# q and k kept in SBUF in 32 bits, masked by head, in an attention block between two half FFNs

## The chip, the cores and the metric

The kernel runs on one core of a Trainium2 chip. The core has TensorE (matmuls, written to PSUM), VectorE, ScalarE, GpSimd, and SyncE, whose queue (SP) issues most of the DMAs; 16 DMA engines move the data. The metric is the device time of one execution in microseconds: lower is better. Before the change the median of two runs is 1265.03 us (1261.8 and 1268.27).

## The reference

The input x has 8 sequences of 1024 tokens with 256 channels. Three layers are added to it one after another: half an FFN, attention, and half of the same FFN, each on a layer-normalized x.

```
r = sigmoid(xr @ W_r.T);  k = xk @ W_k.T;  ffn = r * (relu(k)**2 @ W_v.T)
        # xr, xk: mu * x + (1 - mu) * (x one token earlier)
q, k, v = split(x @ qkv_w.T + qkv_b)             # 16 heads of 16 dims
for i, o in enumerate(OFFSETS):                  # 40 offsets: 0..32, 48, 64, 96, 128, 192, 256, 384
    lg[i] = (q . k shifted by o) / 4 * (1 + q . scale_embed[i]) + pos_bias[i]
p = softmax(lg over the offsets)                 # offsets before the start are masked
out = sum_i p[i] * (v shifted by o_i) * if_gain
x = x + (out * sigmoid(x @ gate_w.T + gate_b)) @ out_w.T + out_b
```

A token thus attends to itself, the 32 tokens before it, and seven tokens farther back.

## The kernel before, in words

Five stages work on different parts of the tokens at the same time: `f1` (first FFN, in chunks of 256 tokens), `p` (projections, chunks of 256), `qk` (scores, by halves of a sequence, 512 tokens), `att` (softmax, values, output projection, tiles of 128) and `f2` (second FFN). Each stage is a generator; the loop at the end takes their steps in an order given by `TRACE` and gives each step a priority by `RANK`. A scheduler then simulates the engines and writes one fixed instruction order for each engine, so the order on an engine isn't that of the text. PSUM has eight banks, one buffer each: `psa` and `psb` for the FFNs, `psp` for the projections, `psq` for scores, `gp`, `pv`, `pst` for transposes in `att`, and `psy` for the transposed output and the output projection.

The steps that the change touches:

- **Projections** (`stage_p`). `proj(w)` computes a 256 x 256 product from two-part operands in fp32r, twelve matmuls into `psp`. For q and k, ScalarE writes `p + bias` in 16 bits (L263), and VectorE the remainder, also in 16 bits (L264); both go in `hl`. Two DMAs per `hl` (L270) write the parts to DRAM (`qk_d`), in an order in which 32 dims of two heads fill 128 partitions, four rows to a dim.
- **Loads for scores** (`stage_qk`). For each half, q is read back as `qst` (L317), two tiles for the two groups `g`, and k in `kb` (L319), which holds the whole sequence, with zeros where the other head of a pair lies. One product over 128 partitions thus gives the scores of two heads with all the cross terms of the two 16-bit parts.
- **Scores** (`scores`, L307). Near scores: 32 queries against 64 keys; four query blocks `a` go to four strips of 32 columns of the array (column tiles), 16 products a call and group. Far scores: queries and keys at a step of 16 tokens, 32 products of 64 columns a call and group in a sequence's first half, 16 of 128 columns in the second. After each call and group ScalarE copies the bank `psq` to `sl` (L308), and DMAs take it to DRAM in a skewed layout, from which `att` reads it by offset.
- **gp** (L403). In `att`, q times the scale embedding, 40 columns, four products for each of two groups and two half sets of heads.
- **Values** (`att`). The exponentials go through DRAM (`pd`) to un-skew them; they are transposed (L464), copied to `ptt`, and multiplied with `vwt` on column tiles into `pv` (32 products a token tile). VectorE divides by the sum; the result is transposed into `psy`, gated in `yt`, and projected in `psy` for every second tile.

All matmuls go through the helper `mm`, so they have the line L134 in the profile, and are told apart by their tiles: p<-kb,qst are the scores, gp<-seb,qst is gp, pv<-vw,ptt the values, p<-xh,wa_hi and the like the projections.

Of the kernel before, what the change touches and what calls it, by code (L numbers as in the profile page):

```python
# [9 lines left out]
F32R = mybir.dt.float32r  # L10
F16 = mybir.dt.float16
I32 = mybir.dt.int32
# [9 lines left out]
LW = 32  # L22
FAR = [384, 256, 192, 128, 64, 96, 48]
ORDER = [LW - u for u in range(LW + 1)] + FAR
NO = len(ORDER)
NL = LW + 1
NF = len(FAR)
# [17 lines left out]
def flat(t, off, *dims):  # L45
    return bass.AP(tensor=t.tensor, offset=off, ap=[list(d) for d in dims])
# [3 lines left out]
def macaron(ctx: ExitStack, tc: tile.TileContext, x, wffn, watt, wo, cols, rows, pbias, se, mask, out):  # L50
# [17 lines left out]
    wa_lo = const.tile([128, 4, 2, 256], F32R, name="wa_lo")  # L68
    seb = const.tile([128, 2, NO], F16, name="seb")
    half = const.tile([128, 4], F32, name="half")  # L70
    nc.gpsimd.memset(half, -0.5)
    kb = [const.tile([128, 4, 2, LW + N], F16, name=f"kb{g}") for g in range(2)]
    vw = [const.tile([128, 4, 2, 8, 17], F32, name=f"vw{i}") for i in range(2)]
# [3 lines left out]
    v_d = [dram.tile([(VPAD + N) * VROW], F32, name=f"vd{i}") for i in range(2)]  # L77
    qk_d = [[dram.tile([256 * 2048], F16, name=f"qk{i}{j}") for j in range(2)] for i in range(2)]

    pstat = pool("pstat", 3)  # L80
    px1 = pool("px1", 13)
    pw = pool("pw", 1)
    ps = pool("ps", 1, space=PSUM)
    pq = pool("pq", 4)
    pvn = pool("pvn", 6)
    psb = pool("psb", 2)
    pga = pool("pga", 5)

# [4 lines left out]
    def load_att():  # L93
        with tc.tile_pool(name="setup", bufs=1) as sp:
            wst = sp.tile([128, 4, 2, 256], F32, name="wst")
            nc.sync.dma_start(wst, watt.rearrange("w (c p) d -> p w c d", p=128))
            nc.vector.tensor_scalar(wst[:, 0], wst[:, 0], 0.25, None, ALU.mult)
            nc.vector.tensor_copy(wa_hi, wst)
            nc.vector.tensor_tensor(wa_lo, wst, wa_hi.bitcast(F32), ALU.subtract)
            nc.vector.tensor_scalar(b_q, b_q, 0.25, None, ALU.mult)  # L100
            nc.vector.tensor_scalar(b_g, b_g, 0.5, None, ALU.mult)
            nc.sync.dma_start(row, rows.unsqueeze(0).to_broadcast([128, 2, 256]))
            for t in [t.bitcast(F32) for t in kb] + vw:
                nc.gpsimd.memset(t, 0.0)
            zero = kb[1].bitcast(F32).rearrange("p a b w -> p (a b w)")
            for i in range(2):
                nc.sync.dma_start(v_d[i][0 : VPAD * VROW].rearrange("(p w) -> p w", p=VPAD), zero[:VPAD, :VROW])
            nc.sync.dma_start(sf_d[0:PADF].rearrange("(p w) -> p w", p=16), zero[:16, : PADF // 16])
            for c0, c1, w in ((0, 8, 384), (8, 15, 384), (15, 16, 368)):
                o = PADF + c0 * ROW + ROW - 384  # L110
                nc.sync.dma_start(flat(sf_d, o, (SF_T, 32), (ROW, c1 - c0), (1, w)), zero[:32, : (c1 - c0) * w])
            nc.sync.dma_start(flat(pd_d, NL * 16, (4 * SKEW, 128), (SKEW, 4), (1, SKEW - NL * 16)), zero[:, : 4 * 512])
            nc.sync.dma_start(bias, pbias.to_broadcast([128, NO * 16]))
            nc.sync.dma_start(msk, mask.rearrange("t p u -> p t u"))
            nc.sync.dma_start(wot, wo.rearrange("(c p) d -> p c d", p=128))
            for c in range(2):
                nc.vector.tensor_scalar(wot[:, c], wot[:, c], gain[:, c : c + 1], 0.5, ALU.mult, ALU.mult)
            se_f = sp.tile([128, NO], F32, name="se_f")
            se_h = sp.tile([128, NO], F16, name="se_h")
            for h2 in range(2):  # L120
                nc.sync.dma_start(se_f[64 * h2 : 64 * h2 + 64], se.unsqueeze(1).to_broadcast([16, 4, NO]))
            nc.vector.memset(seb, 0.0)
            nc.vector.tensor_scalar(se_f, se_f, 4.0, None, ALU.mult)
            nc.vector.tensor_copy(se_h, se_f)
            nc.vector.tensor_tensor(se_f, se_f, se_h, ALU.subtract)
            nc.vector.tensor_scalar(se_f, se_f, slot[:, 1:2], None, ALU.mult)
            for h2 in range(2):
                a = slice(64 * h2, 64 * h2 + 64)
                nc.vector.scalar_tensor_tensor(seb[a, h2], se_h[a], slot[a, 0:1], se_f[a], ALU.mult, ALU.add)

    x1, gate, qs, vn, v3s = {}, {}, {}, {}, {}

# [100 lines left out]
    def stage_p():  # L233
        for c in range(NCH):
# [23 lines left out]

            for j, bb in ((0, b_q), (1, b_k)):
                p = proj(j)  # L260
                for g in range(2):
                    hl = pw.tile([128, 2, 256], F16, name="hl", bufs=4)
                    nc.scalar.activation(hl[:, 0], p[:, g], AF.Identity, bias=bb[:, g : g + 1])  # L263
                    nc.vector.scalar_tensor_tensor(  # L264
                        hl[:, 1], p[:, g], bb[:, g : g + 1], hl[:, 0], ALU.add, ALU.subtract
                    )
                    o = g * 128 * 2048 + cq * 256
                    for r in range(2):
                        ro, s2 = (r * 1024, 512) if j == 0 else (r * 512, 1024)
                        nc.sync.dma_start(flat(qk_d[i % 2][j], o + ro, (2048, 128), (s2, 2), (1, 256)), hl)  # L270
            p = proj(3)
# [25 lines left out]
    def stage_qk():  # L297
        def scores(o, g, q4, q, k, keys):

            p = ps.tile([128, 512], F32, name="p", tag="psq")  # L300
            for pr in range(4):
                for s in range(len(q4(0))):
                    for a in range(4):
                        pp = p[32 * a : 32 * a + 32, pr * 128 : pr * 128 + 128].rearrange("n (h j) -> n h j", h=2)
                        w = 64 // len(q4(a))
                        ms = q4(a)[s]
                        mm(pp[:, :, s * w : s * w + w], q[:, pr, ms], k[:, pr, :, keys(ms)], True, True)  # L307
            nc.scalar.copy(o[:, :, :, g], p.rearrange("n (q h j) -> n j h q", q=4, h=2))  # L308

        for i in range(2 * B):  # L310
            hf = i % 2
            far = sf_d
            for g in range(2):
                kst = kb[g]
                qst = qs[i, g] = pq.tile([128, 4, 512], F16, name="qst")
                o = g * 128 * 2048
                nc.sync.dma_start(qst, flat(qk_d[i % 2][0], o, (512, 128), (32 * 2048, 4), (1, 512)))  # L317
                for h2 in range(2):
                    nc.sync.dma_start(  # L319
                        kst[64 * h2 : 64 * h2 + 64, :, h2, LW + hf * 512 : LW + hf * 512 + 512],  # L320
                        flat(qk_d[i % 2][1], o + h2 * 16 * 2048, (512, 64), (32 * 2048, 4), (1, 512)),
                    )
            ns = 2 - hf
            nth = 4 // ns
            for th in range(nth):
                sf = psb.tile([128, 64, 2, 2, 4], F32, name="sl")
                for g in range(2):
                    scores(
                        sf,
                        g,  # L330
                        lambda a: [slice(c, 512, 16) for c in range((4 * th + a) * ns, (4 * th + a + 1) * ns)],
                        qs[i, g],
                        kb[g],
                        lambda ms: slice(LW + ms.start, LW + (hf + 1) * 512, 16),
                    )
                for a in range(4):
# [13 lines left out]
            for t in range(4):  # L350
                sl = psb.tile([128, 64, 2, 2, 4], F32, name="sl")
                for g in range(2):
                    scores(
                        sl,
                        g,
                        lambda a: [slice(t * 128 + 32 * a, t * 128 + 32 * a + 32)],
                        qs[i, g],
                        kb[g],
                        lambda ms: slice(hf * 512 + ms.start, hf * 512 + ms.start + 64),
                    )  # L360
                for a in range(4):
# [7 lines left out]
    def stage_att():  # L369
        for tt in range(B * NT):  # L370
# [27 lines left out]
            for h2 in range(2):  # L398
                gp = ps.tile([128, 64, 8], F32, name="gp")
                for g in range(2):  # L400
                    for pr in range(4):
                        q = qs[i, g][:, pr, t4 * 128 : t4 * 128 + 128]
                        mm(gp[:, 0:NO, 4 * g + pr], q, seb[:, h2], True, True)  # L403
                e = slice(8 * h2, 8 * h2 + 8)
# [54 lines left out]

            pv = ps.tile([128, 2, 8, 17], F32, name="pv")  # L460
            for g in range(2):
# [124 lines left out]
```

## Time and profile before

| | |
|---|---|
| median of 2 runs | 1265.03 us |
| profiled execution | 1256.76 us, span 1254.0 us |
| granted TensorE clock, mean | 0.956 |
| share of the span busy: TensorE, VectorE, GpSimd, ScalarE | 87%, 75%, 61%, 43% |
| moved by DMA | 282.88 MB, 226 GB/s |
| chain that ended last | TensorE 42%, DMA 25%, VectorE 14%, SP's queue 6%, GpSimd 5% |
| scores: matmul records, busy | 4096, 185.1 us |
| copies of scores, L308 | 224 of 584 ns |
| stores of hl, loads of qst, loads of kb | 256 of 128 KB, 32 of 512 KB, 64 of 256 KB |

A share of busy time counts each moment once, however many instructions of the engine overlap. Matmuls overlap, so what a burst of them costs is read from the start of the first to the start of what follows. A line of the groups has the source line, the engine, the operation, output<-inputs, the shape, the count, and then the busy time and the mean length of one. A line of the timeline has the start, the length and the same names. A line of the waits has who waited for whom, the sum in us, how often, and the longest.

### The profile page before, as it was taken

How to read it: one execution, taken by the hardware profiler on the slowest of the kernel's cores; microseconds unless marked ns; L12 is line 12 of the kernel's file. 1: busy time of each engine (PE TensorE's matmuls, PEld its weight loads, DVE VectorE, ACT ScalarE, POOL GpSimd, SP SyncE). 2: the span in 40 equal slices, each digit the busy share in tenths (PEclk: the TensorE clock that was granted, in tenths of full speed). 3: DMA queues.
4: the chain of work that ended last, by engine and by line, in shares of the span. 5: the costliest groups of instructions: out<-in, count | busy, mean ns of one | idle time of the engine just before them, and what ended most of it. 6: DMA issues, size and time to landing. Idle time of an engine off the chain costs nothing.

```text
span 1254.0 us, 34712 instructions
## 1 busy us (share of the span) xinstructions
PE 1089.2 (87%) x13568; PEld 885.7 (71%) x13568; DVE 942.6 (75%) x2266; ACT 538.0 (43%) x1025; POOL 766.5 (61%) x1101
## 2 busy tenths in 40 slices
PE   2887989899799898989899989899988998888785
PEld 2676768677687677777777778786777787665664
DVE  7546768987587888879678866978858887877772
ACT  2444445344453444536345454544534444524231
POOL 7436619675575656659457564867656755657672
PEclk9999999899999999899999999999989999998988
DMA  8187888786878779787788977797787868998630
GB/s 263 32 224 222 241 242 265 229 238 194 251 226 254 230 233 274 221 252 232 193 260 257 254 201 230 228 269 227 233 243 234 269 197 254 284 280 265 202 99 24
DMA packets 256500, 282.88 MB, mean 226 GB/s; under 512 B 23440, under 2 KB 214608, under 8 KB 256336
## 3 DMA queue, kind: packets, MB, share of 16 engines
q1 hardware_dynamic: 247120, 263.36, 71.7%
q10 hardware_dynamic: 9216, 17.31, 3.8%
q8 instruction: 106, 1.74, 0.6%
q14 instruction: 58, 0.48, 0.1%
HBM read 151.67 MB, written 128.91 MB: 224 GB/s over the span
## 4 chain that ended last, share of the span: by engine, by line
PE 42%; DMA 25%; DVE 14%; SPq 6%; POOL 5%; issue 5%; ACT 4%; POOLq 0%; ACTq 0%; DVEq 0%
PE p L134 29%; DMA pd<-pd 9%; PE tra L464 4%; PE pv L134 3%; PE tra L134 3%; POOL prod L445 2%; DMA lg<-sl 2%; DMA x<-in_x_dram 2%; DMA qk<-hl 2%; DMA kb<-qk 2%; DMA sl<-sl 2%; DVE prod L457 2%; DVE xk L196 1%; PE gp L134 1%; DVE mx L423 1%
## 5 line engine op out<-in xcount | busy, mean ns | idle before, releaser
L134 PEld LDWEIGHTS <-qst 128*32 128x32 f16 (+1 forms) x5120 | 157.2, 120 | 100.1 <-issue 63.5
L134 PE MATMUL p<-kb,qst 128*32 128x128 f16 (+1 forms) x4096 | 185.1, 297 | 12.7 <-ACT sl L308 8.6
L308 ACT COPY sl<-p 128x512 f32<-128x512 f32 x224 | 130.8, 584 | 144.2 <-PE p L134 123.0
L445 POOL TENSOR_TENSOR prod<-v,lg 128x256 f32<-128x256 f32 x248 | 165.5, 687 | 10.2 <-ACT lg L425 6.1
L134 PE MATMUL p<-xk,w_f 128*128 128x256 f32 x512 | 144.9, 421 | 20.0 <-DVE xk L196 11.7
L419 POOL TENSOR_TENSOR lg<-lg,bias 128x640 f32<-128x640 f32 x64 | 113.5, 1774 | 71.8 <-DVE lg L410 66.9
L213 POOL TENSOR_TENSOR x<-x,xr 128x512 f32<-128x512 f32 x64 | 88.4, 1382 | 109.0 <-DVE xr L212 94.9
L457 DVE TENSOR_TENSOR prod<-prod 128x512 f32<-128x512 f32 (+2 forms) x120 | 126.1, 1051 | 32.1 <-POOL prod L445 31.5
L464 PE MATMUL tra<-ident,pd 128*128 128x128 f32 x512 | 97.1, 313 | 58.3 <-DMA pd<-pd 54.9
L160 ACT ACTIVATE xn<-x,nb,y 128x256 f32<-128x256 f32 x192 | 110.8, 602 | 63.0 <-DVE nb L152 55.2
L134 PE MATMUL p<-w_f,xk 128*128 128x256 f32 x512 | 132.9, 400 | 1.7 <-ACT xr L206 1.3
L134 PE MATMUL p<-w_f,xr 128*128 128x256 f32 x512 | 130.4, 396 | 3.6 <-ACT xk L201 2.8
L445 POOL TENSOR_TENSOR prod<-vn,lg 128x256 f32<-128x256 f32 x144 | 96.0, 678 | 54.3 <-ACT lg L425 35.4
L134 PE MATMUL p<-xh,wa_hi 128*128 128x256 f32 x384 | 123.2, 321 | 5.6 <-DVE hl L264 4.4
L134 PEld LDWEIGHTS p<-xk,w_f 128*128 128x128 f32 x512 | 99.3, 208 | 39.8 <-issue 10.5
L470 ACT COPY ptt<-tra 128x512 f32<-128x512 f32 x128 | 74.9, 585 | 116.1 <-PE tra L464 113.0
L464 PEld LDWEIGHTS tra<-ident,pd 128*128 128x128 f32 x512 | 71.0, 197 | 73.9 <-DMA pd<-pd 68.0
L263 ACT ACTIVATE hl<-p,col 128x256 f16<-128x256 f32 x128 | 60.6, 474 | 121.1 <-PE p L134 68.6
L134 PE MATMUL p<-xh,wa_lo 128*128 128x256 f32 x384 | 111.5, 290 | 0.0
L134 PE MATMUL p<-xl,wa_hi 128*128 128x256 f32 x384 | 111.4, 290 | 0.0
L134 PEld LDWEIGHTS p<-w_f,xr 128*128 128x128 f32 x512 | 95.3, 196 | 19.4 <-ACT xk L201 5.8
L134 PEld LDWEIGHTS p<-w_f,xk 128*128 128x128 f32 x512 | 96.0, 198 | 15.9 <-issue 2.8
(82 smaller groups left out, 2394.2 us busy)
## 6 DMA issues: line engine op xcount, KB each, us to landing
qk<-hl SPq DMA_DIRECT2D x256, 128.0 KB, 3.4
sl<-sl SPq DMA_DIRECT2D x256, 128.0 KB, 3.8
pd<-pd SPq DMA_DIRECT2D x64, 512.0 KB, 4.8
sf<-sl SPq DMA_DIRECT2D x184, 128.0 KB, 3.1
vw<-vd SPq DMA_DIRECT2D x128, 136.0 KB, 4.1
v<-vd SPq DMA_DIRECT2D x64, 272.0 KB, 4.3
lg<-sl SPq DMA_DIRECT2D x64, 264.0 KB, 4.1
pd<-lg ACTq DMA_DIRECT2D x64, 264.0 KB, 3.8
```

The lines of the kernel that those rows point to most:

```text
L134: nc.tensor.matmul(o, l, r, start=start, stop=stop)
L160: nc.scalar.activation(xn, x2[:, i], AF.Identity, bias=nb[:, k : k + 1], scale=y[:, k : k + 1])
L196: nc.vector.scalar_tensor_tensor(o[:, h], xr[:, h], mu[:, h : h + 1], prev[:, h], ALU.mult, ALU.add)
L213: nc.gpsimd.tensor_tensor(x2, x2, xr, ALU.add)
L263: nc.scalar.activation(hl[:, 0], p[:, g], AF.Identity, bias=bb[:, g : g + 1])
L308: nc.scalar.copy(o[:, :, :, g], p.rearrange("n (q h j) -> n j h q", q=4, h=2))
L419: nc.gpsimd.tensor_tensor(la, la, bias, ALU.add)
L423: nc.vector.tensor_reduce(mx, lg.rearrange("p u e -> p e u"), AX.X, ALU.max)
L445: nc.gpsimd.tensor_tensor(prod[:, k], shifted[k][1]()[:, :, 0:16], lf[:, k].unsqueeze(2).to_broadcast([128, 16, 16]), ALU.mult,)
L457: nc.vector.tensor_tensor(o, terms[:, 0:m], terms[:, n - m : n], ALU.add)
L464: nc.tensor.transpose(tr[:, pr * 128 : pr * 128 + 128], pd.rearrange("p (m e) -> p m e", e=8)[:, :, 4 * g + pr], ident,)
L470: nc.scalar.copy(ptt.rearrange("p q n -> p (q n)"), tr)
```

## The change

q and k no longer go through DRAM. ScalarE writes each of them from `psp` twice, in 32 bits, with a scale and a bias per partition that are 1 and the bias for some heads and 0 for the others (`qown`, `kown`, `bq2`, `bk2`): q with the two masks of `qown`, k with the two of `kown`. `qst` holds q of a half, `kst` k of a half with 32 keys of the half before in front. A product now takes 64 partitions (`KROW`), so that two row halves `r` of the array write to two PSUM banks, `psq0` and `psq1`. In each, a product has 32 queries against the two masked forms of k; `q` chooses the mask of q. One call covers both groups, and then ScalarE copies the two banks. For the far scores of a second half, the keys lie in two tiles, one product each. `seb` holds the embedding in 32 bits for four heads at a time, so that gp has two products of 80 columns per group and half set. `pv` now uses the bank `psy`, which it shares with the output's transpose and projection. The pools px1 (13 to 12), pga (5 to 4) and pq (4 tiles of a group to 3 of both groups) change, and pk is new with 3.

```diff
-    kb = [const.tile([128, 4, 2, LW + N], F16, name=f"kb{g}") for g in range(2)]
-    px1 = pool("px1", 13)
+    px1 = pool("px1", 12)
-    pq = pool("pq", 4)
+    pq = pool("pq", 3)
+    pk = pool("pk", 3)
-    pga = pool("pga", 5)
+    pga = pool("pga", 4)
...
-            for j, bb in ((0, b_q), (1, b_k)):
-                p = proj(j)
+            if cq == 0:
+                qs[i] = pq.tile([128, 2, 2, 512], F32, name="qst")
+                ks[i] = [pk.tile([128, NK, LW + 512], F32, name=f"kst{g}") for g in range(2)]
                 for g in range(2):
-                    hl = pw.tile([128, 2, 256], F16, name="hl", bufs=4)
-                    nc.scalar.activation(hl[:, 0], p[:, g], AF.Identity, bias=bb[:, g : g + 1])
-                    nc.vector.scalar_tensor_tensor(
-                        hl[:, 1], p[:, g], bb[:, g : g + 1], hl[:, 0], ALU.add, ALU.subtract
-                    )
-                    o = g * 128 * 2048 + cq * 256
-                    for r in range(2):
-                        ro, s2 = (r * 1024, 512) if j == 0 else (r * 512, 1024)
-                        nc.sync.dma_start(flat(qk_d[i % 2][j], o + ro, (2048, 128), (s2, 2), (1, 256)), hl)
+                    pad = ks[i][g][:, :, 0:LW]
+                    if i % 2:
+                        nc.gpsimd.tensor_copy(pad, ks[i - 1][g][:, :, 512 : 512 + LW])
+                    else:
+                        nc.gpsimd.memset(pad, 0.0)
+            for w, dst, own2, own_b in ((0, [qs[i][:, :, g] for g in range(2)], qown, bq2), (1, ks[i], kown, bk2)):
+                p = proj(w)
+                o = cq * 256 + w * LW
+                for g in range(2):
+                    for m in range(2):
+                        nc.scalar.activation(
+                            dst[g][:, m, o : o + 256],
+                            p[:, g],
+                            AF.Identity,
+                            bias=own_b[:, m, g : g + 1],
+                            scale=own2[:, m : m + 1],
+                        )
...
-        def scores(o, g, q4, q, k, keys):
-            p = ps.tile([128, 512], F32, name="p", tag="psq")
-            for pr in range(4):
+        def scores(o, i, q4, keys):
+            pr = [ps.tile([128, 512], F32, name="p", tag=f"psq{r}") for r in range(NR)]
+            for g in range(2):
                 for s in range(len(q4(0))):
                     for a in range(4):
-                        pp = p[32 * a : 32 * a + 32, pr * 128 : pr * 128 + 128].rearrange("n (h j) -> n h j", h=2)
-                        w = 64 // len(q4(a))
-                        ms = q4(a)[s]
-                        mm(pp[:, :, s * w : s * w + w], q[:, pr, ms], k[:, pr, :, keys(ms)], True, True)
-            nc.scalar.copy(o[:, :, :, g], p.rearrange("n (q h j) -> n j h q", q=4, h=2))
+                        for r in range(NR):
+                            pp = pr[r][32 * a : 32 * a + 32].rearrange("n (h g q j) -> n h g q j", h=2, g=2, q=2)
+                            rows = slice(KROW * r, KROW * r + KROW)
+                            ms = q4(a)[s]
+                            for j0, kt, sl_ in keys(ms):
+                                kk = ks[kt][g][rows, :, sl_]
+                                w = kk.shape[2]
+                                for q in range(2):
+                                    o_ = pp[:, :, g, q, s * 32 + j0 : s * 32 + j0 + w]
+                                    mm(o_, qs[i][rows, q, g, ms], kk, True, True)
+            for r in range(NR):
+                nc.scalar.copy(o.rearrange("n j h g q -> n j (h g) q")[:, :, :, 2 * r : 2 * r + 2],
+                    pr[r].rearrange("n (k q j) -> n j k q", k=4, q=2))
...
-                gp = ps.tile([128, 64, 8], F32, name="gp")
+                gp = ps.tile([128, NO, 8], F32, name="gp", tag="gp")
                 for g in range(2):
-                    for pr in range(4):
-                        q = qs[i, g][:, pr, t4 * 128 : t4 * 128 + 128]
-                        mm(gp[:, 0:NO, 4 * g + pr], q, seb[:, h2], True, True)
+                    for q in range(2):
+                        l = qs[i][:, q, g, t4 * 128 : t4 * 128 + 128]
+                        mm(gp[:, :, 4 * g + q : 4 * g + 4 : 2], l, seb[:, h2, :, q:4:2], True, True)
...
-            pv = ps.tile([128, 2, 8, 17], F32, name="pv")
+            pv = ps.tile([128, 2, 8, 17], F32, name="pv", tag="psy")
```

More of the change, by code (lines that the diff above doesn't have):

```diff
@@ L10 @@
 F32R = mybir.dt.float32r
-F16 = mybir.dt.float16
 I32 = mybir.dt.int32
@@ L25 @@
 NO = len(ORDER)
+KROW = 64
+NK = 2
+NR = 128 // KROW
 NL = LW + 1
@@ L68, in macaron @@
     wa_lo = const.tile([128, 4, 2, 256], F32R, name="wa_lo")
-    seb = const.tile([128, 2, NO], F16, name="seb")
+    seb = const.tile([128, 2, NO, 4], F32, name="seb")
+    own = const.tile([128, 8], F32, name="own")
+    kown = const.tile([128, 2], F32, name="kown")
+    qown = const.tile([128, 2], F32, name="qown")
+    bq2 = const.tile([128, 2, 2], F32, name="bq2")
+    bk2 = const.tile([128, 2, 2], F32, name="bk2")
     half = const.tile([128, 4], F32, name="half")
     nc.gpsimd.memset(half, -0.5)
-    kb = [const.tile([128, 4, 2, LW + N], F16, name=f"kb{g}") for g in range(2)]
     vw = [const.tile([128, 4, 2, 8, 17], F32, name=f"vw{i}") for i in range(2)]
@@ L77, in macaron @@
     v_d = [dram.tile([(VPAD + N) * VROW], F32, name=f"vd{i}") for i in range(2)]
-    qk_d = [[dram.tile([256 * 2048], F16, name=f"qk{i}{j}") for j in range(2)] for i in range(2)]
     pstat = pool("pstat", 3)
-    px1 = pool("px1", 13)
+    px1 = pool("px1", 12)
     pw = pool("pw", 1)
     ps = pool("ps", 1, space=PSUM)
-    pq = pool("pq", 4)
+    pq = pool("pq", 3)
+    pk = pool("pk", 3)
     pvn = pool("pvn", 6)
     psb = pool("psb", 2)
-    pga = pool("pga", 5)
+    pga = pool("pga", 4)
     def load_ffn():
@@ L102, in load_att @@
             nc.sync.dma_start(row, rows.unsqueeze(0).to_broadcast([128, 2, 256]))
-            for t in [t.bitcast(F32) for t in kb] + vw:
+            for t in vw:
                 nc.gpsimd.memset(t, 0.0)
-            zero = kb[1].bitcast(F32).rearrange("p a b w -> p (a b w)")
+            zero = sp.tile([128, 4 * 512], F32, name="zero")
+            nc.gpsimd.memset(zero, 0.0)
             for i in range(2):
@@ L110, in load_att @@
                 o = PADF + c0 * ROW + ROW - 384
-                nc.sync.dma_start(flat(sf_d, o, (SF_T, 32), (ROW, c1 - c0), (1, w)), zero[:32, : (c1 - c0) * w])
+                nc.sync.dma_start(flat(sf_d, o, (SF_T, 32), (ROW, c1 - c0), (1, w)), zero[:32, : w].unsqueeze(1).to_broadcast([32, c1 - c0, w]))
             nc.sync.dma_start(flat(pd_d, NL * 16, (4 * SKEW, 128), (SKEW, 4), (1, SKEW - NL * 16)), zero[:, : 4 * 512])
@@ L118, in load_att @@
             se_f = sp.tile([128, NO], F32, name="se_f")
-            se_h = sp.tile([128, NO], F16, name="se_h")
-            for h2 in range(2):
[L121 to L131, printed above, removed]
+            nc.sync.dma_start(se_f, se.unsqueeze(0).to_broadcast([8, 16, NO]))
+            nc.vector.tensor_scalar(se_f, se_f, 4.0, None, ALU.mult)
+            nc.vector.tensor_reduce(
+                own.rearrange("p (h q) -> p h q", h=2),
+                ident.rearrange("p (q h d) -> p h q d", q=4, h=2),
+                AX.X,
+                ALU.add,
+            )
+            nc.vector.tensor_reduce(kown, own.rearrange("p (h q) -> p h q", h=2), AX.X, ALU.add)
+            nc.vector.tensor_reduce(qown, ident.rearrange("p (r q c) -> p q r c", r=2, q=2), AX.XY, ALU.add)
+            for m in range(2):
+                nc.vector.tensor_scalar(bq2[:, m], b_q, qown[:, m : m + 1], None, ALU.mult)
+                nc.vector.tensor_scalar(bk2[:, m], b_k, kown[:, m : m + 1], None, ALU.mult)
+            for h2 in range(2):
+                nc.vector.tensor_tensor(
+                    seb[:, h2],
+                    se_f.unsqueeze(2).to_broadcast([128, NO, 4]),
+                    own[:, 4 * h2 : 4 * h2 + 4].unsqueeze(1).to_broadcast([128, NO, 4]),
+                    ALU.mult,
+                )
+    x1, gate, qs, ks, vn, v3s = {}, {}, {}, {}, {}, {}
     def mm(o, l, r, start, stop):
@@ L257, in proj @@
                 return p
-            for j, bb in ((0, b_q), (1, b_k)):
-                p = proj(j)
+            if cq == 0:
+                qs[i] = pq.tile([128, 2, 2, 512], F32, name="qst")
+                ks[i] = [pk.tile([128, NK, LW + 512], F32, name=f"kst{g}") for g in range(2)]
                 for g in range(2):
-                    hl = pw.tile([128, 2, 256], F16, name="hl", bufs=4)
-                    nc.scalar.activation(hl[:, 0], p[:, g], AF.Identity, bias=bb[:, g : g + 1])
-                    nc.vector.scalar_tensor_tensor(
-                        hl[:, 1], p[:, g], bb[:, g : g + 1], hl[:, 0], ALU.add, ALU.subtract
-                    )
-                    o = g * 128 * 2048 + cq * 256
-                    for r in range(2):
-                        ro, s2 = (r * 1024, 512) if j == 0 else (r * 512, 1024)
-                        nc.sync.dma_start(flat(qk_d[i % 2][j], o + ro, (2048, 128), (s2, 2), (1, 256)), hl)
+                    pad = ks[i][g][:, :, 0:LW]
[7 more added lines that the diff above has]
+                for g in range(2):
+                    for m in range(2):
+                        nc.scalar.activation(
[4 more added lines that the diff above has]
+                            scale=own2[:, m : m + 1],
+                        )
             p = proj(3)
@@ L312, in stage_qk @@
             far = sf_d
[L313 to L322, printed above, removed]
             ns = 2 - hf
@@ L326, in stage_qk @@
                 sf = psb.tile([128, 64, 2, 2, 4], F32, name="sl")
[L327 to L335, printed above, removed]
+                scores(
+                    sf,
+                    i,
+                    lambda a: [slice(c, 512, 16) for c in range((4 * th + a) * ns, (4 * th + a + 1) * ns)],
+                    lambda ms: [(32 * j, i - hf + j, slice(LW + ms.start, LW + 512, 16)) for j in range(hf + 1)],
+                )
                 for a in range(4):
@@ L351, in stage_qk @@
                 sl = psb.tile([128, 64, 2, 2, 4], F32, name="sl")
[L352 to L360, printed above, removed]
+                scores(
+                    sl,
+                    i,
+                    lambda a: [slice(t * 128 + 32 * a, t * 128 + 32 * a + 32)],
+                    lambda ms: [(0, i, slice(ms.start, ms.start + 64))],
+                )
                 for a in range(4):
```

## The prediction

> **What bounds the kernel.** I read the busy times first, then the granted clock, the waits of TensorE, and the timeline of single bursts. The first two lines are from the page, the third is the stretch from 200 to 1000 us, and the last three are from the waits of TensorE:
>
> ```profile
> PE 1089.2 (87%) x13568; PEld 885.7 (71%) x13568; DVE 942.6 (75%) x2266; ACT 538.0 (43%) x1025; POOL 766.5 (61%) x1101
> PEclk9999999899999999899999999999989999998988
> 200.00:1000.00 800.00, 724.07 (x9197) 592.37 (x9199) 635.17 (x1518) 360.83 (x693) 511.80 (x730) 0.96 0.80 237
> PE tra L464 <- DMA pd<-pd: 54.9, 33, 7.2
> PE gp L134 <- DVE lg L410: 10.1, 9, 2.4
> PE gp L134 <- DMA qst<-qk: 3.8, 2, 2.1
> ```
>
> TensorE is busy 724 of 800 us (91%) in the steady part, at a clock of 0.96; VectorE has 79% and the DMA engines 80% there. All TensorE waiting adds up to about 1254.0 - 1089.2 = 165 us, with 55 us of it behind the DRAM round trip of the probabilities and only 3.8 us behind the loads of q that the change removes. So TensorE's work per step sets the pace, and what the change does to it comes first.
>
> The timeline gives the rates (start, length, operation, number of records):
>
> ```profile
> 141.86 1.17 PE L134 MATMUL p<-kb,qst 128*32 128x128 f16 x16
> 142.82 0.25 PE L134 MATMUL pv<-vw,ptt 128*32 128x34 f32 x2
> ...
> 616.06 1.89 PE L134 MATMUL p<-xk,w_f 128*128 128x256 f32 x8
> 617.79 0.45 PE L134 MATMUL gp<-seb,qst 128*128 128x40 f16 x8
> 618.07 0.42 PE L162 MATMUL tr<-ident,xn 128*128 128x128 f32 x2
> ...
> 619.85 0.41 PE L134 MATMUL p<-kb,qst 128*32 128x128 f16 x16
> 620.08 0.65 PE L134 MATMUL pv<-vw,ptt 128*32 128x34 f32 x32
> ...
> 622.68 0.82 PE L162 MATMUL tr<-ident,xn 128*128 128x128 f32 x6
> ...
> 639.30 1.25 PE L134 MATMUL p<-kb,qst 128*32 128x64 f16 x32
> 640.33 0.66 PE L134 MATMUL pv<-vw,ptt 128*32 128x34 f32 x32
> ```
>
> A record's own length includes some 0.2 us in which others run, so I count from a burst's start to the next one's. Near scores: 0.23 us for 16 products, four column tiles at once. Far scores read q and k at a step of 16: 0.96 us for 16 products of 128 columns, or 1.03 us for 32 of 64; that is 0.96/(4 x 128) = 1.9 ns a column with four tiles abreast, where near has 0.23/(4 x 128) = 0.45. A 32-bit product leaves two records (64 tiles x 32 products of pv, but 4096 records); p<-xk has 8 records of 256 columns in 1.73 us, 0.84 ns a column. The transpose, a 128-column 32-bit load for each record, takes (0.82 - 0.29)/5 = 0.106 us (0.29: the mean of one in the groups).
>
> **TensorE, part by part.** Scores and gp cost now: near 64 tiles x 2 halves x 0.23 = 29 us; far 32 bursts x 1.03 + 64 x 0.96 = 94 us; gp 128 bursts x 0.28 = 36 us. Together 159 us.
>
> *gp.* Half the products, 512, but in 32 bits: 1024 records of 80 columns, each behind a load of 128 columns. By columns alone 80 x 0.84 = 67 ns, by the transpose's row 106 ns. I take the transpose, since it has the same load: 1024 x 0.106 = 109 us, **+73** (low end 69 us, +33).
>
> *Near.* 64 calls, each 32 products, 64 records of 128 columns x 0.84 = 108 ns, on 8 tiles (two row halves, four column strips). All eight abreast: 64/8 x 0.108 = 0.86 us a call, 55 us, **+26**. Only two abreast: 3.4 us, 220 us, +191.
>
> *Far.* 48 calls (16 + 32), each 64 products, 128 records of 64 columns. Eight abreast at the 1.9 ns of the strided row: 16 x 64 x 1.9 = 1.95 us, 93 us, **0**. If 32-bit strided reads ran like contiguous ones (0.84): 41 us, -53. Two abreast, sharing the column rate that four tiles have now (so 0.95 ns each): 64 x 64 x 0.95 = 3.9 us, 187 us, +93.
>
> Whether eight run abreast is the open question. In the new order, two products (four in the second half of a sequence) follow each other on the same tile before the next tile's turn. Old scores never do that. The nearest evidence is pv, where each product's two records share a tile: these rows are pv's alone, in 20 ns windows of the burst at 620.08.
>
> ```profile
> 620.08:620.10 0.02, 0.02 (x4) 0.02 (x8) 0.00 (x0) 1.00 0.58 103
> 620.11:620.13 0.02, 0.02 (x8) 0.02 (x9) 0.00 (x0) 1.00 1.54 307
> 620.17:620.19 0.02, 0.02 (x12) 0.02 (x9) 0.00 (x0) 1.00 1.25 256
> 620.24:620.26 0.02, 0.02 (x16) 0.02 (x9) 0.00 (x0) 1.00 0.89 205
> ```
>
> The counts rise by four: four first halves start together, then the four second halves, so a record that waits for its tile doesn't hold back other tiles. That speaks for many abreast, although it shows a look ahead of a few records and the new order needs dozens. The Trainium skill says the opposite: "TensorE: Matmul & The Clock Gate", Part 3, has matmuls in strict program order in start and end. By that rule a second product on a busy tile would stop everything behind it, and TensorE would gain the two-abreast ends above; the quads of pv don't obey it.
>
> *Mode switches.* In the compiled order, runs of scores, of pv and of full-array work alternate 855 times; now it is 676, where scores and pv count as one mode. The run of 32 pv at 620.08 has its last start at 620.08 + 0.65 - 0.23 (a record's mean length) = 620.50, and full-array work begins at 620.85: 0.35 us, less the 0.06 that pv's next four would take, so a switch costs 0 to 0.29 us. I take the middle: 179 x 0.14 = **+25** (0 to 52).
>
> Sum on TensorE: 73 + 26 + 0 + 25 = **+124 us**.
>
> **What gets easier.** 256 stores of hl, 32 loads of qst and 64 of kb go, 67 of 283 MB, and with them 256 x 0.54 + 32 x 0.37 + 64 x 0.62 = 190 us of issuing on SP's queue, which is 6% of the chain that ended last. 128 VectorE operations of 472 ns (60 us) go too. TensorE's waits for the loads and for hl are 3.8 + 1.6 + 4.4 = 10 us; they vanish. For the wait behind pd I take half of 55, 27 us, as the transfers meet less traffic and more TensorE work lies between; of 31 us behind lg, acc and xk (VectorE) a third, 10 us. Sum **-47** (none to -75).
>
> **Moved without cost.** ScalarE gets 128 more ACTIVATEs of 474 ns (+61 us), but is at 43%. The projection's bank psp is freed after four of them (1.9 us), where two ACTIVATEs and a last VectorE step took 1.4; 64 x 0.5 = 32 us if nothing else were ready; the FFN matmuls are. Each scores call now ends in two copies of 584 ns in a row before its banks are free, instead of one: up to 112 x 0.58 = 65 us uncovered, against 8.6 us that TensorE waits for these copies today; I cost it at 0. pv waits for the output projection of the step before: its bank is held some 6 us of a 19.6 us step, so 0, or 64 x 1 us if steps crowd. GpSimd gets 32 paddings of about 0.3 us and loses two memsets of 3.6 us at the start; the setup's small VectorE steps, a dozen for seven of 0.1 to 0.2 us, end before the first projection needs them. One gate buffer and one x buffer less: the compiled order keeps gates 5 to 8 half chunks ahead, 5 to 8 before, so 0.
>
> Sum on the profiled execution: span 1254.0 + 124 - 47 = 1331, and 2.8 us that lie around it: **1334 us**, 6% over that execution's 1256.8. The median of the two runs shown, 1265, is 8 us above it. I predict 1335. A measurement here tells about 2% from no change.
>
> **Rivals.**
> *Tiles block each other.* Same-tile products stop the queue and about two tiles run abreast: 73 + 191 + 93 + 25 = +382, less 47: 1592 us. For it: the new order's runs on one tile. Against: pv's quads. With four abreast, near is 110 us (+81) and far stays at 93: +179, 1389 us.
> *The transfers were the limit: not slower.* gp at its 67 ns (+33), near +26, far unpenalised (-53), switches +25: TensorE only +31, and waits fall by 47: 1241 us, 2% under the median; with waits down 75 it is 1213. It decides from the point where TensorE's growth stays under what its waits lose, here 47 to 75 us. For it: 25% of the chain is DMA. Against: TensorE is already busy 91% of the steady part.
> *Evacuation becomes the wait.* The forecast plus 65 us of uncovered copies: 1399 us, seen as TensorE waiting for the scores' copy.
>
> **How the numbers follow.** Forecast, 1280 to 1370: 0.42. Four abreast or uncovered copies, 1370 to 1430: 0.18. Blocked tiles, 1430 to 1600: 0.18. Not slower, 1205 to 1280: 0.22, with 0.13 under 1240. The range leaves out the lowest tenth and the worst tenth: 1230 to 1560. Faster by over 2% 0.13, within 0.12 (1240 to 1290 holds a sliver of the forecast), slower 0.75.
>
> **What would show it.** TensorE should stay the busiest, near 90%, with about 1200 us; gp records at 106 ns pitch; a near burst of 64 records in 0.9 us (3.4 if tiles block); a far one of 128 in 2 us. VectorE should lose 60 us, the DMA share fall from 0.76 (71.7% + 3.8% + 0.7%) towards 0.76 x 216/283 x 1254/1331 = 0.55, and pd's wait shrink. I am wrong if burst pitches lie at either end, or if TensorE waits on the copies.

## The result

| | median, us | runs | ratio to before (95% interval) |
|---|---|---|---|
| before | 1265.03 | 2 | |
| changed | 1572.34 (1571.31 to 1573.37) | 2 | 1.243 (1.229 to 1.257) |

The change makes the kernel 24% slower. The forecast was 1335, between 1230 and 1560: the direction was right, the size far off, and the result lies 12 us outside the range. The rival "tiles block each other", at 1592, was the nearest, and it had less than a fifth of the chance.

The profiled execution took 1571.31 us, span 1569.5. Three views of it answer to those shown of before. First its page, with the busy time of each engine and the granted clock:

```profile
PE 1465.1 (93%) x19712; PEld 1252.1 (80%) x19712; DVE 881.8 (56%) x2141; ACT 611.7 (39%) x1153; POOL 743.8 (47%) x1132
PEclk9999989999999989999999999999999999999977
```

Then the stretch from 200 to 1200 us (its length; busy time of PE, PEld, VectorE, ScalarE, GpSimd; granted clock, DMA share, GB/s):

```profile
200.00:1200.00 1000.00, 950.94 (x12912) 814.65 (x12913) 577.26 (x1390) 402.68 (x763) 486.90 (x732) 0.98 0.47 139
```

And from the list of waits, the one behind pd (total us, number of waits, the longest):

```profile
PE tra L483 <- DMA pd<-pd: 28.4, 22, 3.0
```

TensorE has 376 us more work (1465.1 - 1089.2) and waits 60 us less (1569.5 - 1465.1 = 104.4, against 164.8); 376 - 60 is the whole growth of the span, 1569.5 - 1254.0 = 315.5. Most of the rest got easier, as forecast: VectorE lost 61 us (ScalarE gained 74), the DMA share in the steady part fell from 0.80 to 0.47, and the wait behind pd from 55 to 28 us. The clock didn't suffer. The next lines, groups by shape, say whose work it is (before the bar the count, after it the busy time and the mean length of one record):

```profile
L151 PE MATMUL p<-kst,qst 64*32 64x64 f32 x6144 | 347.2, 290 | 0.0
L151 PE MATMUL gp<-seb,qst 128*128 128x80 f32 x1024 | 146.8, 280 | 10.3 <-DVE mv L160 7.2 <-DVE lg L429 1.7 <-DVE rc L500 1.3
L151 PE MATMUL p<-kst,qst 64*32 64x128 f32 x4096 | 143.5, 275 | 0.3 <-ACT sl L342 0.3
```

The scores were busy for 185.1 us before and are now for 347.2 + 143.5 = 490.7: +306. gp went from 65.0 to 146.8: +82. Together these are 388, and all the rest fell by 12, which makes the 376. The timeline of the changed kernel shows single bursts (start and length in us; the number of records stands behind the x):

```profile
591.78 1.51 PE L151 MATMUL p<-kst,qst 64*32 64x64 f32 x62
593.22 0.70 PE L151 MATMUL pv<-vw,ptt 128*32 128x34 f32 x32
...
615.01 1.47 PE L151 MATMUL p<-kst,qst 64*32 64x128 f32 x64
616.41 1.12 PE L151 MATMUL gp<-seb,qst 128*128 128x80 f32 x8
617.37 0.63 PE L483 MATMUL tra<-ident,pd 128*128 128x128 f32 x4
...
712.39 8.09 PE L151 MATMUL p<-kst,qst 64*32 64x64 f32 x128
720.41 0.71 PE L483 MATMUL tra<-ident,pd 128*128 128x128 f32 x4
```

A near burst of 64 records takes 1.40 us to the next one's start, where 0.86 was forecast. A piece of a far burst in a sequence's first half has 62 records in 1.44 us: 23 ns each, 15 forecast. A far burst in a second half, 128 records, takes 8.02 us, where 1.95 was forecast. It is the same shape as the first half's, 64 columns at a step of 16, but it has 63 ns a record. What differs is the order: in second halves four products (eight records) lie on one tile before the next tile's turn, in first halves and in near bursts two (four records).

### The profile page after: what moved, and what is told of

The parts are those of the page before. It is cut to its first block, busy times and chain, and to the rows that moved or that the text cites. A ratio compares the mean times of both kernels' runs of the same rounds, so it can differ in the third digit from the quotient of the medians.

```text
span 1569.5 us, 46503 instructions
## 1 busy us (share of the span) xinstructions
PE 1465.1 (93%) x19712; PEld 1252.1 (80%) x19712; DVE 881.8 (56%) x2141; ACT 611.7 (39%) x1153; POOL 743.8 (47%) x1132
## 4 chain that ended last, share of the span: by engine, by line
PE 67%; DVE 12%; DMA 10%; POOL 5%; ACT 3%; issue 3%; SPq 1%; POOLq 0%; ACTq 0%; DVEq 0%
PE p L151 49%; PE gp L151 5%; DMA pd<-pd 4%; PE pv L151 4%; PE tra L483 4%; POOL prod L464 3%; PE tr L179 2%; DVE prod L476 2%; PE tra L151 2%; DVE xk L213 2%; DMA x<-in_x_dram 2%; DMA out_dram<-x 1%; DVE mx L442 1%; DVE st L159 1%; DVE xr L210 1%
## 5 line engine op out<-in xcount | busy, mean ns | idle before, releaser
L151 PE MATMUL p<-kst,qst 64*32 64x64 f32 (+1 forms) x10240 | 490.7, 284 | 0.3 <-ACT sl L342 0.3
L151 PEld LDWEIGHTS p<-kst,qst 64*32 64x32 f32 x10240 | 401.1, 123 | 61.9 <-issue 40.9
L464 POOL TENSOR_TENSOR prod<-v,lg 128x256 f32<-128x256 f32 x248 | 154.5, 643 | 42.2 <-ACT lg L444 42.2
L438 POOL TENSOR_TENSOR lg<-lg,bias 128x640 f32<-128x640 f32 x64 | 105.3, 1646 | 125.0 <-DVE lg L429 105.7
L151 PE MATMUL gp<-seb,qst 128*128 128x80 f32 x1024 | 146.8, 280 | 10.3 <-DVE mv L160 7.2
L151 PEld LDWEIGHTS gp<-seb,qst 128*128 128x128 f32 x1024 | 133.5, 195 | 27.9 <-issue 21.1
L151 PE MATMUL p<-xk,w_f 128*128 128x256 f32 x512 | 136.2, 406 | 8.7 <-DVE xk L213 4.4
L424 DVE SCALAR_TENSOR_TENSOR lg<-gp,lg 128x264 f32<-128x264 f32 x128 | 54.6, 427 | 144.2 <-PE gp L151 134.3
L151 PE MATMUL p<-w_f,xk 128*128 128x256 f32 x512 | 127.3, 391 | 2.6 <-ACT xr L223 2.6
L224 POOL TENSOR_TENSOR xk<-xk 128x512 f32<-128x512 f32 x64 | 75.6, 1181 | 95.0 <-ACT xk L218 94.6
L483 PE MATMUL tra<-ident,pd 128*128 128x128 f32 x512 | 92.4, 302 | 28.4 <-DMA pd<-pd 28.4
```

The costliest lines, as they stand in the source:

```text
L151: nc.tensor.matmul(o, l, r, start=start, stop=stop)
L224: nc.gpsimd.tensor_tensor(xk, xk, xk, ALU.mult)
L424: nc.vector.scalar_tensor_tensor(lg[:, 0:NL, e], gp[:, 0:NL], 1.0, lg[:, 0:NL, e], ALU.add, ALU.mult)
L438: nc.gpsimd.tensor_tensor(la, la, bias, ALU.add)
L464: nc.gpsimd.tensor_tensor(prod[:, k], shifted[k][1]()[:, :, 0:16], lf[:, k].unsqueeze(2).to_broadcast([128, 16, 16]), ALU.mult,)
L483: nc.tensor.transpose(tr[:, pr * 128 : pr * 128 + 128], pd.rearrange("p (m e) -> p m e", e=8)[:, :, 4 * g + pr], ident,)
```

## The experiments

### 1. Only the order of the products

e1_tiles_inner has the changed kernel's products, tiles and copies; the loops are exchanged so that neighbours go to eight different tiles. e2_rows_inner only puts the two row halves inside the loops over key tiles and masks.

```diff
 # e1_tiles_inner                                   # e2_rows_inner
-for g: for s: for a: for r: for key: for q:        -for g: for s: for a: for r: for key: for q:
+for g: for s: for key: for q: for a: for r:        +for g: for s: for a: for key: for q: for r:
     mm(o_, qs[i][rows, q, g, ms], kk, True, True)
```

> The changed kernel with only the order of the score products changed: the four column strips and the two row halves are the innermost loops, so that eight products in a row go to eight different tiles. Theory (TensorE looks ahead over some 16 products' halves, so products that follow each other on one tile keep the other tiles idle): a near burst of 64 records falls from 1.40 us to 0.9, a far one of 128 from 8.0 us (second halves) or 3.7 (first halves) to 2.0; the scores' TensorE time falls by about 280 us and the median to 1290, between 1250 and 1340. Rival (32-bit products, or 32-bit reads at a step, are slow in any order): the bursts keep their length, and the median stays over 1500.

> The changed kernel with the two row halves innermost, so that neighbours always lie on different tiles, but a strip still gets all its products before the next strip's turn. Theory (what counts is how many tiles the look ahead reaches): the same number of products stands between one strip and the next, so nothing changes, 1540 to 1600. Rival (only a product directly behind another on the same tile blocks): most of what the tile order costs is won back, 1250 to 1400.

e1 took 1431.92 us (1.129 of before, 1.120 to 1.139), e2 1502.24 (1.182, 1.172 to 1.191). e1's page, the line of busy times:

```profile
PE 1286.4 (90%) x19712; PEld 1061.7 (74%) x19712; DVE 886.2 (62%) x2141; ACT 612.8 (43%) x1153; POOL 740.6 (52%) x1132
```

e1's far scores in the groups by shape (count, busy time, mean ns):

```profile
L151 PE MATMUL p<-kst,qst 64*32 64x64 f32 x6144 | 162.6, 313 | 2.2 <-issue 1.5 <-ACT kst L290 0.7
```

e1's timeline, a far burst and a near one:

```profile
118.19 2.81 PE L151 MATMUL p<-kst,qst 64*32 64x64 f32 x128
120.93 0.55 PE L151 MATMUL pv<-vw,ptt 128*32 128x34 f32 x18
...
655.89 1.16 PE L151 MATMUL p<-kst,qst 64*32 64x128 f32 x64
656.98 0.78 PE L151 MATMUL gp<-seb,qst 128*128 128x80 f32 x5
```

e2's timeline, a far burst:

```profile
118.74 5.60 PE L151 MATMUL p<-kst,qst 64*32 64x64 f32 x128
124.27 0.44 PE L179 MATMUL tr<-ident,xn 128*128 128x128 f32 x2
```

The order alone is worth 140 us. The far scores' busy time falls from 347 to 163 us, and TensorE's by 179. A near burst takes 1.09 us, which is the 0.86 forecast for eight tiles abreast and 0.23 in which the last ones run out; a far one 2.74 (1.95 forecast; what makes the other 0.8, beside running out, isn't shown). So it isn't 32-bit products at a step as such that made a far burst take 8 us. But e1 missed its expected 1290 by 140 us: that is the subject of part 3.

e2 refutes the theory as I had stated it. Near bursts stayed as they were, but a far burst fell from 8.0 to 5.53 us and the median by 70 us, where I expected nothing. It isn't the rival's 1250 to 1400 either. A theory that fits most of it is that instructions are handed out in order, that each tile can hold only a few of them, and that one too many for a full tile stops all that come behind it. Four records a tile then fit (near, first halves: six and five abreast on average, by 108/17.5 and 125/23, with 17.5 ns a record in (1.40 - 0.28)/64, where 0.28 is one record's length, and 125 = 64 x 1.95); eight don't, and the next tile's turn comes only when half of them are done: two abreast, 125/63. With the row halves alternating (e2), both halves fill at the same time, so it should be four abreast; measured are 125/43 = 2.9, which the theory leaves open.

### 2. Is it the number in a row?

Three runs ask that of other products. e3 gives it to the kernel before, where near scores and second halves have four products of two instructions (a load and a matmul) each for every strip, and first halves eight. e10 is e1 with the near scores alone put back to four 32-bit products (eight records) a tile. e11 is the changed kernel with the far reads side by side instead of at a step.

```diff
 # e3_before_strip_outer
-for pr in range(4):              +for a in range(4):
     for s in range(len(q4(0))):       for s in range(len(q4(0))):
-        for a in range(4):       +        for pr in range(4):
 # e10_near_four, near scores only
-for g: for s: for key: for q: for a: for r:
+for a: for r: for g: for q:
 # e11_after_far_contiguous (also e7_far_contiguous, on e1)
-lambda a: [slice(c, 512, 16) for c in ...
+lambda a: [slice(c * 32, c * 32 + 32) for c in ...
-slice(LW + ms.start, LW + 512, 16)
+slice(LW + ms.start, LW + ms.start + 32)
```

> The kernel before with the strip outermost: a strip gets its four (near, far of second halves) or eight products (far of first halves) in a row. Theory (a look ahead of some 16 products): four products a strip still leave four strips in reach, so near bursts keep 0.23 us and far ones of second halves 0.96; eight a strip leave two strips, but these already share the column rate of strided reads. 1255 to 1300. Rival (strict program order of matmuls): near and far bursts take about three times as long, 29 and 94 us become 90 and 250 at most, 1380 to 1480.

> The order of e1_tiles_inner for the far scores; in the near scores each tile gets its four products, eight records, in a row. Theory, formed from the runs so far (TensorE hands out instructions in order, each tile holds about four records, and a fifth for the same tile stops the handing out): two tiles run abreast, a near burst of 64 records takes 64/2 x 0.108 + 0.28 = 3.7 us, where two products a tile took 1.40 and one 1.09; the near scores' TensorE time rises from 115 us to some 270. Rival (a look ahead of a fixed number of records over all tiles, some 16 to 24): between two and three abreast, 2.4 to 3.7 us. Rival (only far bursts of second halves are slow, by their reads at a step or their two key tiles): 1.4 us.

> The changed kernel with the far scores reading 32 neighbouring tokens instead of every sixteenth, so the far scores are those of other pairs; the order of products is the changed kernel's. Theory (a tile holds about four records): second halves still run two abreast, 64/2 x 0.054 + 0.3 = 2.0 us for 64 records where the step gives 4.27; first halves some six abreast, 0.9 us where it is 1.5. Rival (the second halves are slow through the step of their reads alone): they become as fast as the first ones, 0.9 us.

e3: 1298.55 us (1.024, 1.016 to 1.031). e10: 1533.11 in one run, e11: 1490.91 in one run, beside a median of 1256.74 for the kernel before. The timeline of e3, a near burst and a first half's far one, each up to the next work:

```profile
190.27 0.44 PE L134 MATMUL p<-kb,qst 128*32 128x128 f16 x16
190.63 1.99 PE L134 MATMUL tra<-wot,yt 128*128 128x256 f32 x8
...
194.58 2.64 PE L134 MATMUL p<-kb,qst 128*32 128x64 f16 x32
197.15 1.99 PE L134 MATMUL p<-w_f,xr 128*128 128x256 f32 x8
```

e10's timeline, a near burst:

```profile
181.45 3.88 PE L151 MATMUL p<-kst,qst 64*32 64x128 f32 x64
185.26 0.45 PE L151 MATMUL pv<-vw,ptt 128*32 128x34 f32 x14
```

e11's timeline, far bursts of a second half and of a first half:

```profile
116.91 4.43 PE L151 MATMUL p<-kst,qst 64*32 64x64 f32 x128
121.27 0.70 PE L151 MATMUL pv<-vw,ptt 128*32 128x34 f32 x32
...
894.71 1.02 PE L151 MATMUL p<-kst,qst 64*32 64x64 f32 x64
895.66 0.71 PE L483 MATMUL tra<-ident,pd 128*128 128x128 f32 x4
```

All three follow the number in a row, whatever the type or the reads. In e3 the near burst with four products a strip keeps its length (0.44, it was 0.41), and the first half's with eight takes 2.57 us instead of 1.03; over the whole run the first halves' scores are busy for 88.7 us instead of 42.0, the others, four in a row, for 153.4 instead of 143.1. In e10 the near burst takes 3.81 us; 3.7 was expected, and 1.40 and 1.09 are what two products and one product a tile take. Only the near scores moved, and the run is 101 us slower than e1. In e11 second halves still have 4.36/128 = 34 ns a record against 0.95/64 = 15 in first halves, although no read is at a step. That e11's second halves became faster at all (8.02 to 4.36 us) is the step's own price, 1.95 against 0.84 ns a column.

So the number of records in a row on one tile decides how many tiles run abreast. Whether each tile holds about four, or all tiles together some sixteen, the lengths don't tell apart: e10 fits the first reading's 3.7 us, and the second's 2.4 to 3.7 nearly. The changed kernel's trace does. These rows count the score records that ran in stretches (the x) of the near burst at 615.01 and of the second half's far burst at 712.39:

```profile
614.99:615.46 0.47, 0.45 (x32) 1.00 0.93 240
712.38:712.85 0.47, 0.46 (x4) 1.00 1.05 423
712.38:712.88 0.50, 0.49 (x6) 1.00 0.99 398
```

In the near burst 32 records run within the first 0.47 us; at 0.108 us a record that takes eight tiles with four each, although in the order as written the eighth tile's first record is the 29th. In the far burst only four run in that time, one after another as on one tile. Then two more start within 0.03 us: the first tile's fifth and, by this reading, the first of the next tile, which is the ninth in order. One limit of sixteen for all tiles would forbid the first and allow more in the second; about four for each tile fits both. The near burst, then, isn't six abreast throughout: half of it runs eight abreast, and the other half takes 0.93 us.

e3 also corrects a price. I had let two strided streams share the column rate of four (0.95 ns a column). Two abreast in e3 take 2.57 us for 16 pairs of 64 columns, 2.5 ns a column, with running out; in the changed kernel 2 x 63/64 = 1.96. So some 1.9 ns is a stream's own, with one at work (the four records above, 0.47/(4 x 64) = 1.8), with two, or with four (before). For the eight of e1 it isn't shown: 2.74 us for 16 x 64 columns a tile is 2.7 ns, with running out.

### 3. What keeps the good order at 1432

With e1, TensorE's work is 197 us over before (1286.4 - 1089.2), and its waits are 22 us under: 175 us, the difference of the spans. Of the 197, gp has 84 (149.0 - 65.0) and the scores 104 (289.4 - 185.1). Whole bursts would give 64 x 1.09 + 48 x 2.74 = 201 us. The planner cuts them: 347 runs of scores for 112 calls. e5 keeps calls whole; e6 halves gp's loads; e7 is e1 with far reads side by side.

```diff
 # e5_whole_calls
+with tc.high_priority(6000):
     for g: for s: for key: for q: for a: for r:
 # e6_wide_gp: the products of q's second mask are left out
-for q in range(2):
-    mm(gp[:, :, 4 * g + q : 4 * g + 4 : 2], qs[i][:, q, g, ...], seb[:, h2, :, q:4:2], True, True)
+mm(gp[:, :, 4 * g : 4 * g + 4], qs[i][:, 0, g, ...], seb[:, h2], True, True)
```

> The order of e1_tiles_inner, and the scores' products get a higher priority in the planner, so that a call's products stay together: 125 runs of scores on TensorE in the compiled order, where e1 has 347. Theory (a piece of a call costs a full product's two halves and a drain whatever it holds, 0.36 us for under 16 records against 1.09 for a whole near call of 64): the scores' TensorE time falls from 268 us to some 190, the median from 1432 to 1370, between 1335 and 1400. Rival (pieces cost only their records): 1420 or more.

> The order of e1_tiles_inner, with gp in half as many products of 160 columns instead of 80; only q under its first mask is used, so half the heads get no scale term. The columns are the same, the 128-column loads of q are halved. Theory (a 32-bit load sets gp's pace, 122 ns a record): 512 records of some 138 ns, gp's TensorE time falls from 128 to 70 us, the median from 1432 to 1385, between 1365 and 1405. Rival (columns or the writes to PSUM set it): gp keeps its 128 us, within 1% of 1432.

> The order of e1_tiles_inner, with the far scores reading 32 neighbouring tokens of q and k instead of every sixteenth, so the far scores are those of other pairs. Theory (the step of the reads sets the far bursts' pace, 1.9 ns a column against 0.84): a burst of 128 records falls from 2.45 us to 1.15, the far scores' TensorE time from 152 us to 90, the median from 1432 to 1380, between 1355 and 1405. Rival (the step costs nothing in 32 bits): within 1% of 1432.

| | median, us | ratio to before (95%) | TensorE busy, us | span less busy, us | scores busy, us |
|---|---|---|---|---|---|
| e1 | 1431.92 | 1.129 (1.120 to 1.139) | 1286.4 | 142.9 | 289.4 |
| e5 | 1429.36 | 1.134 (1.130 to 1.138) | 1242.1 | 186.6 | 232.5 |
| e6 | 1364.08 | 1.082 (1.077 to 1.087) | 1224.0 | 136.9 | 284.7 |
| e7 | 1419.65 | 1.126 (1.118 to 1.134) | 1251.4 | 174.0 | 235.4 |

Two of the three miss by far (e6 lies 1 us under its range). e5 and e7 took work off the scores (57 and 54 us less) and off TensorE (44 and 35 us less), and waits took nearly all of the latter back (44 and 31 us). In e5 TensorE's list of waits has (total us, number, the longest):

```profile
PE gp L151 <- DVE lg L431: 21.6, 15, 5.4
...
PE p L151 <- ACT sl L344: 12.3, 9, 3.9
```

gp behind VectorE and the scores behind their own copies are new; e1 has none of them over 6 us. A whole call needs both its banks, and what stood between its pieces now stands behind it. So pieces cost TensorE time, but they were also what filled its gaps. In e7 20 of the 31 us stand behind pd (71.7 us, against 51.3 in e1). The granted clock differs as well: 0.93 to 0.94 in e5's four runs, where e1 has 0.95 to 0.96; and of e7's four, two took 1411 and 1412 us at 0.95, and two, the profiled one among them, 1427 and 1429 us at 0.93 to 0.94. How much of the missing gain is the clock isn't told apart, and why e6 kept its gain I can't show.

e6 answers half of its question: with the same columns and half the 128-column loads, gp's busy time falls from 149 to 101 us, by the groups of e6's page:

```profile
L151 PE MATMUL gp<-seb,qst 128*128 128x160 f32 x512 | 101.4, 319 | 8.3 <-DVE lg L429 6.1
```

So the columns don't set the pace of the changed kernel's gp: 0.96/8 = 120 ns a record at 80 columns (616.41 to 617.37 above), where columns alone would need 67. In e6 they do, with 0.54/4 = 135 ns for 160 columns (602.61 to 603.15 in its timeline; 160 x 0.84 = 134). That it is the load that sets the 120 ns is likely, but not shown: the changed kernel's gp also reads seb and writes to PSUM at a step of two, and e6 does neither.

### 4. Parts tried on the kernel before

The one part of the change that stands alone is the shared bank (e4). e8 gives the bank that it frees to the scores, and e12 keeps calls whole.

```diff
 # e4_before_pv_psy, and in e8 and e12
-pv = ps.tile([128, 2, 8, 17], F32, name="pv")
+pv = ps.tile([128, 2, 8, 17], F32, name="pv", tag="psy")
 # e8_before_two_banks
-p = ps.tile([128, 512], F32, name="p", tag="psq")
+p = ps.tile([128, 512], F32, name="p", tag="psq", bufs=2)
 # e12_before_psy_whole
+with tc.high_priority(2000):
     for pr in range(4):
```

> The kernel before with the values in the bank of the output's transpose and projection, the one part of the change that can be made alone. Theory: the bank is free in time, within 1% of the kernel before. Rival (the shared bank holds up the values of the next tile): up to 1 us for each of 64 tiles, 1300 to 1330.

> The kernel before with the values in the bank of the output projection, and the bank this frees as a second one for the scores, so that products and copies alternate. Theory (TensorE waits 8.6 us for copies and its order is cut up by them): a little faster than with the shared bank alone (1258), 1225 to 1255. Rival (the copies were hidden already): 1250 to 1268.

> The kernel before with the values in the bank of the output projection (e4_before_pv_psy, 1258 us), and a higher priority for the scores' products, 242 runs of scores in the compiled order where e4 has 308. Theory (TensorE's work falls a little, and its waits rise as they did in e5_whole_calls): no gain, 1250 to 1290. Rival (whole calls save switches at no cost): 1225 to 1250.

e4: 1257.91 us, 0.992 of before (0.989 to 0.996). The shared bank costs nothing that shows in the time, though pv now waits 8.2 us for the readers of its bank; and this is the one version with a median below both kernels', by 0.8%. e8: 1283.86 (1.018, 1.013 to 1.022): a second bank for the scores, which I expected to help, makes it no faster, and by its median slower, just under the 2% that are told from no change. e12: 1271.18 (1.012, 1.005 to 1.020), no gain, as expected. Each of these edits makes the planner write a new order for every engine; the loads of k, which come through DRAM here, now hold up the scores for 28.8 us in e8, where it was 1.6. The 0.8% of e4 may come from such a new order as well, or from the clock: its runs had 0.953 in the mean, those of before beside it 0.946, and six others of before, at 0.951, have a median of 1256.74. That isn't shown.

## Why the prediction was wrong, step by step

- **What bounds the kernel**: right. TensorE stayed the busiest engine, at 95% of the steady part, and the span grew by its added work less what its waits gave up.
- **gp, +73**: the size was right, +82, with 120 ns a record; the reason isn't shown. The transpose's 106 ns, taken as the price of a load, is also what its 128 columns cost (128 x 0.84 = 107), so that row couldn't tell the two apart; and the step of two in gp's reads and writes wasn't counted.
- **Near, +26, eight abreast**: the step that failed. A whole burst takes 1.40 us, not 0.86; 64 of them make 90 us.
- **Far, 0, eight abreast**: failed, and cost most. Second halves take 32 x 8.02 = 257 us where 32 x 1.95 = 62 was counted. The inference behind both was that pv's quads show that a record waiting for its tile doesn't hold back the others. They show it for two records a tile; the new order has four, and in second halves eight. I noted that the look ahead shown was a few records and the order needs dozens, and still took the far end as the likeliest. The rule of strict program order in the Trainium skill ("TensorE: Matmul & The Clock Gate", Part 3) doesn't hold here either: in the near burst eight tiles are at work at once with four records in a row on each, and in second halves the next tile begins with the fifth of eight. The prediction took the two-abreast ends for what that rule gives, but by it only a tile's last record would run beside the next tile's first: 16 x 7 x 0.125 = 14 us for a second half's burst, an estimate, where 8.02 was measured.
- **Two abreast, far +93**: mis-sized even as the rival's end. Two strided streams don't share four streams' rate; two abreast cost 257 us in the second halves alone. That the rival's 1592 came within 20 us is luck: its near scores, 220 us, were 130 too long, and its far ones, 187 us, some 120 too short (257 and 16 first halves of about 3.0 us).
- **Switches, +25**: not measured by itself. What pieces of bursts cost shows in e5: 57 us of the scores' busy time between 347 and 125 runs, of which TensorE as a whole kept 44, and the waits took those back.
- **Waits, -47**: the size was right, -60; the DMA share, VectorE's 61 us and pd's wait went as forecast. That lighter traffic shortens pd's wait isn't shown: e1 moves as many bytes and waits 51.3 us behind pd, where the changed kernel has 28.4 and before 54.9. More TensorE work in between, the other argument, doesn't account for it alone either, since e1 has 197 us more than before; what shortened the wait stays open.
- **Copies, banks, gates, at 0**: right. TensorE's scores wait 0.3 us for their copies, and e4's time shows no cost of the shared bank.
- **The chances**: the direction was right, but the blocked tiles had 0.18, and the range was cut at 1560, below that rival's own 1592.

## What to carry to other kernels

When products go to row and column tiles, the order in which they are issued is part of their price: change tile with every product, and put what must follow on the same tile as far apart as it goes. Here eight records in a row on a tile left two tiles at work, four some six on average, and two (one 32-bit product) all eight in the near burst; the same products took 3.81, 1.40 and 1.09 us. And less work on the busiest engine isn't yet less time under a planned order: 35 to 44 us came off TensorE in two runs and the waits took most of them back, while the 62 us of e6 came through whole, so each such edit has to be measured as a whole.

## What the runs showed of the hardware

- Several tiles of the array run independently, and TensorE's records don't start in strict order, but a tile with more than about four records ahead stops the rest. It happened with 16-bit products on four strips (1.03 to 2.57 us) as with 32-bit ones on eight tiles (1.09 to 3.81 us).
- Reads at a step of 16 elements take 1.9 to 2.0 ns a column for each stream, in 16 bits (32 bytes apart) with four streams at once as in 32 bits (64 bytes apart) with two, and 1.8 in 32 bits with one. A 32-bit contiguous record takes 0.84. In second halves, doing away with the step took 8.02 to 4.36 us.
- gp's records, each behind a load of 128 columns, come 120 ns apart in 32 bits (80 columns, read and written at a step of two) and came 35 ns apart in 16 bits (40 columns, 0.28/8 before). The 120 ns aren't the columns, and likely the load; the step isn't ruled out.
